# A six-layer decoder on one Trainium2 core: reordered turns in two 16-head attentions, whole projections, and stage ends run beside the next stage

## The chip, the cores and the metric

The kernel is one program on one core of a Trainium2 chip. Its metric is the device time of one execution in microseconds (us), as the median of three runs; lower is better.

A core has five engines with queues of their own: TensorE (PE, with weight loads shown as PEld), VectorE (DVE), ScalarE (ACT), GpSimd (POOL) and SyncE (SP, which here only issues DMAs). Each works through its own list of instructions in a fixed order; they meet through semaphores. PE's results go to PSUM, which the kernel divides into eight banks of 128 x 512 fp32.

## The reference

All is fp32, with eight sequences of 256 tokens and 256 features. Six sublayers follow each other, each as `x = layernorm(x + f(x))`:

1. a gated convolution and state layer; 2. a cross attention, 16 heads of 64, over 77 context rows; 3. a mixture of eight experts (two per token) with a shared one; 4. a self-attention, 16 heads of 16, with rotary position; 5. a cross attention as 2; 6. a self-attention, 16 heads of 16, with two key sets:

```python
sim = (qg_n[None, None] * q_n).sum(-1).mean(-1)
sim = (sim - sim.min()) / (sim.max() - sim.min())
pos = sim > 0.9
...
x_pos = masked_attn(pos)
x_neg = masked_attn(~pos)
reg_out = (x_pos[:, :REG] + x_neg[:, :REG]) * 0.5
tok_out = jnp.where(pos[:, :, None, None], x_pos[:, REG:], x_neg[:, REG:])
```

The first five tokens (`REG`) are registers. The minimum and the maximum of `sim` are over tokens, so the last attention's masks need every token of sublayer 5.

## The kernel before

The change touches sublayers 4 to 6. Tensors stay in SBUF, batch by batch (b = 0 to 7, 256 tokens), as rows (`x_s`) and turned (`xT_s`).

**A scheduler and hand-written order.** The program is written as a trace of instructions; a scheduler fixes each engine's list beforehand from its own estimates. `tc.issue_after(ins)` keeps what is written inside behind `ins` on the same engine. In the two 16-head attentions PE's order is so bound by hand (`bound`); in the cross attention and between stages the scheduler chooses.

**Heads16** is shared by sublayers 4 (`Rotary`) and 6 (`split`). One turn i handles one of four groups of four heads of a batch, 32 turns in all. Its four heads' matmuls have 32 rows each and lie on four strips of the array (`tile_position`). In turn i:

- `scores(i)` (L1032): queries times keys into two bank pairs; DVE takes the row maxima (L1038).
- `products(i-2)` (L1080): exponentials times values, with sums of them in a spare column, into the bank `op`; ACT copies it out (L1087).
- place 0: the first half of a projection, of values or of an output block, in the bank `mm`.
- `exponentials(i-1)` (L1061): scores again, turned, with the maximum subtracted through a spare row; ACT's exp (L1069).
- place 1: the second half of that block; place 2: a side block in `op`, which DVE empties (turning a finished batch, L89 and L94, or the register tokens' steps, L1496, L1520, L1530).
- `turn_maxima(i)` (L1048): the maxima turned into `op`; DVE adds them to the queries (`shifted`, L1188 or L1403).
- place 3: copies out of `mm`, and DVE's and POOL's work on older turns.

PSUM holds one `op`, one `mm` and three bank pairs `sc`, taken in turn by scores and exponentials. For the division, `products` sends the sums by DMA into a compact 128 x 16 tile (`comp`, L1091), `inverted` takes the reciprocal (L1098) and sends it back (L1100), and `normed` spreads and multiplies it (L1108 to L1112). The output block of batch b stands at turn 4b+10 (4b+8 for the last).

**Rotary** projects batch b+1 while batch b is attended (turns 4b, 4b+1, 4b+3) and turns a finished batch two turns after its output. When all turns are through, its pools close.

**cross** begins with keys (L375, L384, L446), values, weighted keys (L457) and weighted values (L411), and then goes through 16 units of scores (L476), turning (L505) and outputs (L521). What a stage leaves over is handed to the next one as a list `tail` of pieces.

**Signs** gathers, after each batch of the second cross attention, `sim` from a projection (L1343) and a power on POOL (L1357). `positive` takes the extremes over the tokens: DVE reduces along the rows, POOL across the partitions:

```python
nc.vector.tensor_reduce(e2, ext, AX.X, ALU.max)
e3 = s1.tile([P, 2], F32, name="e3")
nc.gpsimd.partition_all_reduce(e3, e2, P, bass_isa.ReduceOp.max)
```

**split** (sublayer 6) starts with 15 "early" blocks (queries, keys, values of five batches) in `sc` banks, ACT copying half of the queries (L1435) and DVE the other half (L1438); the signs are turned (L1645), stored to DRAM and spread from there by small DMAs (`marked`, L1454) into spare rows of queries and keys. The other three batches are projected in turns 8 to 19.

Of the kernel before, what the change touches and what calls it, by code (L numbers as in the profile page):

```python
# [18 lines left out]
P = 128  # L19
# [31 lines left out]
def decoder_kernel(ctx: ExitStack, tc: tile.TileContext, a: dict, out: bass.AP):  # L51
# [281 lines left out]
    def cross(xs, W, bias, ctxT, at_unit, after, tail):  # L333
# [10 lines left out]
        with ExitStack() as st:  # L344
            c1 = st.enter_context(pool_of(tc, name="c1", bufs=1))
# [208 lines left out]
            places = (1, 1, 4, 5, 5, 6, 6)  # L554
# [397 lines left out]
    class Heads16:  # L952
# [12 lines left out]
        def __init__(self, st, queries, keys, shifted):  # L965
# [19 lines left out]
            nc.gpsimd.tensor_scalar(self.second, self.second, cs["slot"][:, 1:2], None, ALU.add)  # L985
            self.qs, self.pT, self.o, self.comp, self.oT = ({} for _ in range(5))
# [14 lines left out]
        def project(self, w, col, xT_b, ps, halves=(0, 1)):  # L1001

            for c in halves:
                for kc in range(2):
                    nc.tensor.matmul(  # L1005
                        ps[:, c * SEQ : (c + 1) * SEQ],
                        w[:, kc, col + c * P : col + (c + 1) * P], xT_b[:, kc, :],
                        start=kc == 0, stop=kc == 1,
                    )

        def values(self, xT_b, wv, ps, halves=(0, 1)):
            for kb in halves:
                for kc in range(2):
                    nc.tensor.matmul(
                        ps[:, kb * D : (kb + 1) * D], xT_b[:, kc, kb * P : (kb + 1) * P],
                        wv[:, kc, :], start=kc == 0, stop=kc == 1,
                    )
# [56 lines left out]
        def products(self, i):  # L1074
# [9 lines left out]
            if m == 0:  # L1084
                self.o[b, c] = self.c2.tile([P, 2, SEQ], F32, tag="o", name="o")
            o = self.o[b, c]
            nc.scalar.copy(o[:, m], ps[:, :SEQ])  # L1087

# [16 lines left out]
        def normed(self, b, c):  # L1105
            o = self.o.pop((b, c))
            wide = self.c2.tile([P, SEQ], F32, tag="wide", name="wide", bufs=1)
            nc.vector.stream_shuffle(wide, self.rows[c], [i // 16 * 16 for i in range(32)])  # L1108
            nc.vector.copy_predicated(o[:, 0], self.second.bitcast(U32), o[:, 1])
            if c == 0:  # L1110
                self.oT[b] = self.c2.tile([P, 2, SEQ], F32, tag="oT", name="oT")
            nc.vector.tensor_tensor(self.oT[b][:, c], o[:, 0], wide, ALU.mult)  # L1112

        def out(self, oT, w, ps, halves=(0, 1)):
            for j in halves:
# [11 lines left out]
        def run(self, events):  # L1127
# [12 lines left out]
            for i in range(max(max(e[0] for e in events) + 1, n + 2)):  # L1140
                if i < n:
                    bound(self.scores, i)
                with tc.issue_after(self.last.ins):
                    if 0 <= i - 2 < n:
                        bound(self.products, i - 2)
                    for f in events.get((i, 0), ()):
                        bound(f)
                    with ExitStack() as st:
                        if 0 <= i - 1 < n:
                            st.enter_context(  # L1150
                                tc.issue_after(bound(self.exponentials, i - 1).ins)
                            )
                        for f in [*events.get((i, 1), ()), *events.get((i, 2), ())]:
                            bound(f)
                        if i < n:
                            bound(self.turn_maxima, i)
                        for f in events.get((i, 3), ()):
                            f()


    class Rotary:
# [34 lines left out]
        def project(self, b, i, ps, halves=(0, 1)):  # L1196
            self.at.project(self.W[0], i * 256, self.xT_of(b), ps, halves)
# [25 lines left out]
        def values(self, b, ps, halves=(0, 1)):  # L1223
            self.at.values(self.xT_of(b), self.W[1], ps, halves)
# [18 lines left out]
        def run(self, st, bias, tail):  # L1243
            at, xs, done, sums, banks = self.at, self.xs, [], {}, {}
            at.open(st)
            events = {}

            def put(i, place, f, *args):
                events.setdefault((i, place), []).append(lambda: f(*args))

            def halves(i, f, *args):

                def half(h):
                    if h == 0:
                        banks[i] = at.mm()
                    f(*args, banks[i], (h,))

                for h in range(2):
                    put(i, h, half, h)

            def emptied(i, f, *args):
                put(i, 3, lambda: f(*args, banks.pop(i)))

            def turn_out(b, ps, copy=None):
                s, half = divmod(b, 2)
                transposed(
                    ps, done[s][0][:, half * 2 : half * 2 + 2, :], done[s][1], half, copy
                )
# [11 lines left out]
            def finish(b):  # L1280
# [3 lines left out]
                normed(sums.pop(b), done[s][0][:, half * 2 : half * 2 + 2, :], nc.gpsimd)  # L1284

            for b in range(NB):
                t = 4 * b
                for c in range(2):
                    put(t + 4 + 2 * c, 3, at.inverted, b, c)
                    put(t + 5 + 2 * c, 3, at.normed, b, c)  # L1290
                put(t + 7, 3, biased, b)
                o = t + (10 if b < NB - 1 else 8)
                halves(o, lambda b, ps, h: at.out(at.oT[b], self.W[2], ps, h), b)
                emptied(o, added, b)
                put(o + 1, 3, finish, b)
                if b < NB - 1:
                    put(o + 2, 2, lambda b: turn_out(b, at.side(), nc.vector.tensor_copy), b)
                n = b + 1
                if n < NB:
                    for k, i in ((0, 1), (1, 0)):  # L1300
                        halves(t + k, self.project, n, i)
                        emptied(t + k, self.projected, n, i)
                        put(t + k + 1, 3, self.rotate, n, i)
                    halves(t + 3, self.values, n)
                    emptied(t + 3, self.valued, n)
            for k, piece in enumerate(tail):
                put(k, 2, lambda piece: piece(at.side(), nc.vector.tensor_copy), piece)
            at.run(events)
            return done, [lambda ps: turn_out(NB - 1, ps)]


    class Signs:
# [49 lines left out]
        def positive(self):  # L1362
# [11 lines left out]
            nc.vector.tensor_reduce(e2, ext, AX.X, ALU.max)  # L1374
            e3 = s1.tile([P, 2], F32, name="e3")
            nc.gpsimd.partition_all_reduce(e3, e2, P, bass_isa.ReduceOp.max)
# [10 lines left out]
    def split(xs, W, bias, signs, cs, tail):  # L1387
        wqkv, wo = W
        wv = wqkv[:, :, 512:768]
        with ExitStack() as st:  # L1390
# [33 lines left out]
            def project(b, i, ps, halves=(0, 1)):  # L1424
                at.project(wqkv, i * 256, xT_of(b), ps, halves)

            def projected(b, i, ps):
                v = ps.rearrange("p (c t) -> p c t", c=2)
                if i == 1:
# [8 lines left out]
                nc.vector.tensor_scalar(  # L1438
                    qms[b][:, 1], v, cs["scaled"][:, 1:2], None, ALU.mult
                )  # L1440

            def values(b, ps, halves=(0, 1)):
                at.values(xT_of(b), wv, ps, halves)
# [5 lines left out]
            def marked(tile, b, k0):  # L1449


                for m in range(2):
                    for k in range(2):
                        nc.sync.dma_start(  # L1454
                            out=tile[at.free[m] + 1 + k :: 32, m],
                            in_=sgr[k0 + k : k0 + k + 1, b].partition_broadcast(4)
                            .to_broadcast([4, 2, SEQ]),
                        )
# [11 lines left out]
            def mark_queries(b):  # L1470
                marked(qms[b], b, 0)

            def mask(b):

                marked(kps[b % 2], b, 2)
# [17 lines left out]
            def registers_scores(b):  # L1493
                qd, sc = rg[b], at.side()
# [22 lines left out]
            def registers_turn(b):  # L1517
                sl, tr = rg[b][0], at.side()
# [7 lines left out]
            def registers_products(b):  # L1526
                pn, vn, on = rg.pop(b), vns.pop(b), at.side()
# [36 lines left out]
            events = {}  # L1564

            def put(i, place, f, *args):
                events.setdefault((i, place), []).append(lambda: f(*args))

            def halves(i, f, *args):

                def half(h):
                    if h == 0:
                        banks[i] = at.mm()
                    f(*args, banks[i], (h,))

                for h in range(2):
                    put(i, h, half, h)

            def emptied(i, f, *args):
                put(i, 3, lambda: f(*args, banks.pop(i)))  # L1580

            for b in range(NB):
                t = 4 * b
                put(t, 2, registers_scores, b)
                put(t, 3, registers_exponentials, b)
                put(t + 1, 3, registers_normed, b)
                put(t + 2, 2, registers_turn, b)
# [290 lines left out]
```

## Time and profile before

| | us |
|---|---|
| median of three runs (1419.97 to 1421.14) | 1420.35 |
| the profiled execution | 1418.84 |
| its span | 1417.1 |
| PE busy | 1337.2 (94%) |
| DVE busy | 784.0 (55%) |
| ACT busy | 490.9 (35%) |
| POOL busy | 423.7 (30%) |

The span runs from the first to the last instruction of the profiled execution. In lines of the timeline the columns are start and length in us, engine, line of the kernel, operation, what is written from what with partitions x elements, the number of instructions put together, and in brackets the idle time before them with what ended it. PE's ends are modelled, so distances between starts are the safer reading.

### The profile page before, as it was taken

To read this page: it belongs to the slowest core of one execution; us is meant where nothing else is said; L and a number is where in the kernel's file an instruction comes from. 1 tells how busy PE (TensorE), PEld (TensorE's weight loads), DVE (VectorE), ACT (ScalarE), POOL (GpSimd) and SP (SyncE) were. 2 spreads that over 40 slices of the span, in tenths; PEclk is the share of its full clock that TensorE was granted. 3 is DMA by queue.
4 is the path that set the end of the run, shared out by engine and by line. 5 is a ranking of instruction groups with operands and counts; after the bars stand their busy time and mean duration, and the time that the engine had idled before them with its cause. 6 is when DMAs were issued, how large, how long until landed. Compare 5 with 4: busy or idle time off the path is not lost.

```text
span 1417.1 us, 21778 instructions
## 1 busy us (share of the span) xinstructions
PE 1337.2 (94%) x8518; PEld 916.2 (65%) x8518; DVE 784.0 (55%) x1505; ACT 490.9 (35%) x734; POOL 423.7 (30%) x470
## 2 busy tenths in 40 slices
PE   8999999999999999999989999799999987999884
PEld 3555578888866666656556665578887875555552
DVE  3776465555643223324657777455655653766773
ACT  3455633243331022221134444343233312444441
POOL 0100012131200133246335575412453452122422
PEclk9999999999999999999999999999999998999996
DMA  8000053335240022242120000043222200000000
GB/s 277 6 1 0 1 165 91 107 91 159 96 193 0 24 74 89 79 138 67 38 83 3 3 3 3 2 156 109 88 74 78 71 0 12 15 21 16 23 11 23
DMA packets 80201, 88.22 MB, mean 62 GB/s; under 512 B 14564, under 2 KB 74884, under 8 KB 79588
## 3 DMA queue, kind: packets, MB, share of 16 engines
q1 hardware_dynamic: 76692, 77.53, 17.4%
q0 software_dynamic: 3408, 9.31, 2.3%
q8 instruction: 68, 1.11, 0.3%
q14 instruction: 33, 0.27, 0.1%
HBM read 56.77 MB, written 29.52 MB: 61 GB/s over the span
## 4 chain that ended last, share of the span: by engine, by line
PE 71%; DVE 6%; POOL 3%; issue 2%; DMA 2%; ACT 1%; SPq 0%; another core or an unknown queue 0%; POOLq 0%; DVEq 0%; ACTq 0%
PE mm L521 9%; PE sc L476 8%; PE mm L779 7%; PE ps_sc L1032 5%; PE mm L842 5%; PE ps_sc L1061 5%; PE op L1080 4%; PE tr L796 3%; PE ps_mm L1117 3%; PE ps_mm L1005 3%; PE tr L856 2%; PE sc L505 2%; PE sc L375 2%; PE sc L457 2%; PE sc L411 2%
## 5 line engine op out<-in xcount | busy, mean ns | idle before, releaser
L1038 DVE TENSOR_REDUCE mx<-ps_sc 128x4 f32<-128x1024 f32 x128 | 150.8, 1221 | 39.2 <-PE ps_sc L1032 39.1
L1069 ACT ACTIVATE pT<-ps_sc 128x1024 f32<-128x1024 f32 x128 | 124.1, 1021 | 97.0 <-PE ps_sc L1061 97.0
L496 POOL TENSOR_TENSOR p<-p,sm 128x616 f32<-128x616 f32 x60 | 72.7, 1217 | 242.9 <-DVE sm L493 216.3
L521 PE MATMUL mm<-Ub,pT 128*128 128x256 f32 (+1 forms) x640 | 144.6, 379 | 0.5 <-ACT pT L75 0.4
L476 PE MATMUL sc<-M,xT_s 128*128 128x308 f32 x512 | 138.9, 423 | 1.1 <-ACT pT L75 1.1
L521 PEld LDWEIGHTS mm<-Ub,pT 128*128 128x128 f32 (+1 forms) x640 | 120.8, 190 | 20.0 <-ACT pT L75 0.9
L779 PE MATMUL mm<-xT_s,w 128*128 128x512 f32 x256 | 115.1, 602 | 3.3 <-DVE h L785 3.3
L476 PEld LDWEIGHTS sc<-M,xT_s 128*128 128x128 f32 x512 | 94.4, 188 | 35.3 <-ACT pT L75 2.1
L489 ACT ACTIVATE p<-p 128x616 f32<-128x616 f32 x64 | 45.9, 717 | 154.4 <-DVE p L485 132.7
L779 PEld LDWEIGHTS mm<-xT_s,w 128*128 128x128 f32 x256 | 48.4, 192 | 58.2 <-issue 54.2
L1061 PE MATMUL ps_sc<-qs,kp 32*128 32x256 f32 x1024 | 82.9, 411 | 0.6 <-DVE mx L1038 0.6
L816 POOL DMA_INDIRECT xb<-xd,token x39 | 37.3, 956 | 146.2 <-PE tr L823 81.0
L1080 PE MATMUL op<-pT,va 128*32 128x256 f32 x1024 | 74.4, 405 | 5.0 <-DVE qs L1188 2.2
L483 DVE TENSOR_REDUCE nmx<-sc 128x8 f32<-128x616 f32 x64 | 51.1, 799 | 46.2 <-PE sc L476 46.2
L842 PE MATMUL mm<-wE,xbT 128*128 x156 | 73.5, 593 | 0.3 <-ACT xbT L828 0.3
L1061 PEld LDWEIGHTS ps_sc<-qs,kp 32*128 32x128 f32 x1024 | 52.9, 189 | 28.4 <-issue 23.9
L114 POOL TENSOR_SCALAR rstd<-mv 128x2 f32<-128x2 f32 x48 | 11.8, 245 | 175.2 <-DVE mv L112 175.2
L492 DVE TENSOR_REDUCE sm<-p 128x8 f32<-128x616 f32 x64 | 50.6, 790 | 22.2 <-ACT p L489 21.9
L1087 ACT COPY o<-op 128x256 f32<-128x256 f32 x64 | 23.8, 372 | 111.7 <-PE op L1080 111.7
L181 PE MATMUL pair<-xT_s,w 128*128 128x512 f32 x128 | 57.9, 612 | 0.9 <-DMA w<-in_W_inT 0.9
L254 PE MATMUL pair<-xc,w 128*128 128x512 f32 x128 | 58.6, 600 | 0.0
L828 DVE COPY hT<-tr 128x256 f32<-128x256 f32 x39 | 16.6, 425 | 75.7 <-PE tr L823 75.7
(293 smaller groups left out, 2459.3 us busy)
## 6 DMA issues: line engine op xcount, KB each, us to landing
Ub<-ud SPq DMA_DIRECT2D x32, 512.0 KB
ud<-U SPq DMA_DIRECT2D x16, 616.0 KB
wE<-in_wE SPq DMA_DIRECT2D x4, 1536.0 KB
yd<-y SPq DMA_DIRECT2D x39, 128.0 KB
Ub<-ud SPq DMA_DIRECT2D x32, 104.0 KB
ud<-U SPq DMA_DIRECT2D x4, 608.0 KB
x_s<-in_x SPq DMA_DIRECT2D x8, 256.0 KB
w<-in_Wo SPq DMA_DIRECT2D x2, 1024.0 KB
```

The source lines that it names most:

```text
L181: last = nc.tensor.matmul(ps[:, i, :], w_in[:, kc, c * P : (c + 1) * P], xT_s[:, kc, :], start=kc == 0, stop=kc == 1,)
L254: last = nc.tensor.matmul(ps[:, i, :], w_dt[:, kc, c * P : (c + 1) * P], xc[s][kc // 2][:, kc % 2, :], start=kc == 0, stop=kc == 3,)
L476: nc.tensor.matmul(sc[:, a, : 4 * NCTX], xT_b[:, kc, j * P : (j + 1) * P], M[:, a * 4 : a * 4 + 4, kc, at : at + NCTX], start=kc == 0, sto ...
L496: engine.tensor_tensor(pv, pv, bcast(sm, 2, [P, 8, NCTX]), ALU.mult)
L521: nc.tensor.matmul(o[:, j * D : (j + 1) * D], pT[:n, c, j * P : (j + 1) * P],  Us[b][:n, g, c], start=g == 0 and j == 0 and c == 0, stop=g ...
L779: nc.tensor.matmul(ps, w[:, kc, cols], xT_s[:, kc, :], start=kc == 0, stop=kc == 1)
L842: nc.tensor.matmul(ps, xT[:, kc, :], column(j, kc * 512, 512), start=kc == 0, stop=kc == 1)
L1032: nc.tensor.matmul(scs[s // 2][:, s % 2, qb * SEQ : (qb + 1) * SEQ], self.queries(b, c, s, m)[:, qb * P : (qb + 1) * P], self.keys(b, c, s ...
L1038: self.last = nc.vector.tensor_reduce(self.mx[m][:, :, 2 * j : 2 * j + 2, self.free[m]].rearrange("p q s -> p s q"), scs[j].rearrange("p s ...
L1061: nc.tensor.matmul(scs[s // 2][:, s % 2, kb * SEQ : (kb + 1) * SEQ], self.keys(b, c, s, m)[:, kb * P : (kb + 1) * P], qs[s * 32 : (s + 1) ...
L1069: last = nc.scalar.activation(pT[:, 2 * j : 2 * j + 2].rearrange("p s k t -> p s (k t)"), scs[j], AF.Exp)
L1080: nc.tensor.matmul(ps[s * 32 : (s + 1) * 32, :SEQ], va[:, kb, 8 * c + 2 * s + m, :], pT[:, s, kb, :], start=kb == 0, stop=kb == 1, tile_po ...
```

## The change

It does these things:

- **Order within a turn**: scores, products, exponentials, the side block (now place 0), a whole block in `mm` (place 1), maxima, then copies and the rest (place 2). The halves go.
- **What falls after the last turn** is not run in further turns but returned, with the step that closes the rotary pools, as pieces for the cross attention to run: three after its first keys, three after its first values, the last after the first weighted values. The cross attention's first pool lies at the other end of SBUF (`side="right"`), and `o`, `oT`, `wide` in a pool that stays open.
- **The last batch's division** in both attentions goes without DMA: the sums are copied where they lie, a reciprocal is taken of 128 x 256, and the shuffle fetches them from the other half of each 32 rows.
- The output of batch 6 stands at turn 32, not 34; the rotary's last batch is scaled by DVE, not POOL; its turned copies are DVE's.
- **Signs**: the extremes across partitions come from a PE transpose, a DVE maximum, and a matmul with ones that spreads them.
- **split**: another order of the early blocks, with the tail's two pieces and the signs' two steps between them; early queries copied by ACT alone; the marking DMAs of one batch and half for queries and keys together, first half first; projections of the last three batches at turns 5, 9, 13; 11, 15, 17; 19, 21, 23.

The core of the diff:

```diff
@@ Heads16.products / normed
+            if b == NB - 1:
+                return
...
+                rows = self.rows[c]
+                nc.vector.tensor_copy(rows, o[:, 1])
+                nc.vector.copy_predicated(rows, second, o[:, 0])
+                nc.vector.reciprocal(rows, rows)
+                nc.vector.stream_shuffle(wide, rows, [(i + 16) % 32 for i in range(32)])
@@ Heads16.run
-            for i in range(max(max(e[0] for e in events) + 1, n + 2)):
+            for i in range(n + 2):
                 if i < n:
                     bound(self.scores, i)
-                with tc.issue_after(self.last.ins):
+                with tc.issue_after(self.last.ins), ExitStack() as st:
                     if 0 <= i - 2 < n:
                         bound(self.products, i - 2)
-                    for f in events.get((i, 0), ()):
-                        bound(f)
...
+                    if 0 <= i - 1 < n:
+                        st.enter_context(tc.issue_after(bound(self.exponentials, i - 1).ins))
+                    for f in work.pop((i, 0), ()):
+                        bound(f, self.side())
+                    ends = []
+                    for f, end in work.pop((i, 1), ()):
+                        ps = self.mm()
+                        bound(f, ps)
+                        ends.append(lambda end=end, ps=ps: end(ps))
+                    if i < n:
+                        bound(self.turn_maxima, i)
+                    for f in ends + work.pop((i, 2), []):
+                        f()
+            rest = []
...
+            return rest
@@ Rotary.run, and split likewise
-                o = t + (10 if b < NB - 1 else 8)
+                o = t + (10 if b < NB - 2 else 8)
...
+            return done, rest[:-1] + [lambda ps: close(), rest[-1]]
@@ Signs.extremes, positive
+            nc.tensor.transpose(ps[:2, :P], e2, ident)
+            most = s1.tile([P, 1], F32, name="most")
+            nc.vector.tensor_reduce(most[:2], ps[:2, :P], AX.X, ALU.max)
...
+            nc.tensor.matmul(ps[:, :2], ones[:2], self.both[:2], start=True, stop=True)
             e3 = s1.tile([P, 2], F32, name="e3")
-            nc.gpsimd.partition_all_reduce(e3, e2, P, bass_isa.ReduceOp.max)
+            nc.vector.tensor_copy(e3, ps[:, :2])
@@ split
+            at_turn = ((5, 9, 13), (11, 15, 17), (19, 21, 23))
...
+            turn_last, add_last = tail
+            for i in range(3):
+                early(0, i)
+            fill(0)
+            turn_last(at.mm())
+            early(1, 0)
+            add_last(at.mm())
+            for i in range(1, 3):
+                early(1, i)
+            fill(1)
+            for i in range(3):
+                early(2, i)
+            early(3, 0)
+            signs.extremes(at.side())
+            early(3, 1)
+            pos = signs.positive(at.side())
...
+            early(3, 2)
...
+            for b in range(2):
+                mask(b, True)
@@ the second cross attention
-            lambda b, n_s, nT_s, ps: signs.add(b, nT_s, ps), tail,
+            lambda b, n_s, nT_s, ps: signs.add(b, nT_s, ps), tail, (0, 0, 0, 1, 1, 1, 4), "right",
```

## The prediction

> **What bounds the kernel now.** I read the page first (PE is busy for 94% of the span and has 71% of the chain that ended last), then the busy times by stretch, then the list of PE's waits, then the timeline of single turns and of the three places where one stage hands over to the next. The stretches are: rotary turns, start of the second cross attention, its end with the start of the last attention, the last attention's turns, the end.
>
> ```profile
> 712.00:912.00 200.00, 183.85 (x1874) 116.95 (x1875) 139.43 (x257) 85.39 (x118) 103.60 (x111) 0.98 0.06 17
> 912.00:950.00 38.00, 36.88 (x311) 31.22 (x310) 19.22 (x31) 16.76 (x25) 12.43 (x10) 1.00 0.33 105
> ...
> 1148.00:1210.00 62.00, 50.00 (x256) 38.61 (x258) 21.70 (x46) 14.81 (x26) 18.82 (x18) 0.86 0.03 9
> 1210.00:1390.00 180.00, 161.63 (x1716) 99.16 (x1720) 125.65 (x246) 77.92 (x114) 51.17 (x73) 0.97 0.07 16
> 1390.00:1417.00 27.00, 10.91 (x48) 6.14 (x48) 6.84 (x21) 2.59 (x4) 4.52 (x6) 0.63 0.09 29
> ```
>
> The columns are stretch, length, busy time of PE, PE's loads, DVE, ACT, POOL, then PE's granted clock, DMA share and GB/s. PE idles 16 us in the rotary turns, 12 and 18 us in the last attention, 16 us at the end, and where it idles its clock falls (0.86, 0.63), so idle time is paid twice.
>
> A turn on PE, from start to start, is scores S (L1032), products P (L1080), exponentials E (L1061), maxima turned T (L1048), and in some turns a matmul block M (projection, values or output) and a side block X. I number turns by the starts of L1032 and take lengths from one start to the next. In the rotary turn that begins at 780.27 (turn 12, 6.93 long):
>
> ```profile
> 783.41 1.15 PE L1061 MATMUL ps_sc<-qs,kp 32*128 32x256 f32 x16
> ...
> 785.45 0.60 PE L89 MATMUL op<-ident,x_s 128*128 128x128 f32 x4
> 786.09 0.69 DVE L94 COPY xT_s<-op 128x512 f32<-128x512 f32 x1 [2.12 <-PE op L89]
> ...
> 786.84 0.44 PE L1048 MATMUL op<-ident,mx 128*128 128x128 f32 x2 [0.79 <-DVE xT_s L94]
> ```
>
> T needs the one `op` bank, which DVE must first empty, so 1.38 us pass from X to T (PE's waits name this xT_s nine times, 8.6 us). And turn 28, without M:
>
> ```profile
> 876.15 1.51 PE L1061 MATMUL ps_sc<-qs,kp 32*128 32x256 f32 x16
> 877.60 0.66 PE L89 MATMUL op<-ident,x_s 128*128 128x128 f32 x4
> ```
>
> Here E takes 1.45 from start to start, not 1.08: its second bank pair is the first one of S, and DVE's first maximum (1.22 us, begun 0.03 after S ends) is not done when only P (1.00) lies between. A half M (1.06) before E covers that today. Behind a waiting E stand X, M and T on PE, and ACT's exponentials.
>
> **Order within a turn and whole projections.** Before: S 1.08, P 1.00, half M 1.06, E 1.08, half M 0.97, X, T 0.31. After: S, P, E, X, whole M, T. A whole M is 1.83 (713.79 to 715.62, eight matmuls together), 0.20 less than two halves. E loses its cover and takes 1.45.
> Turn with M alone: before 5.49; after 1.08+1.00+1.45+1.83+0.31 = 5.67, so +0.18. Turn with X and M: before 6.93; after X lasts 0.50 and DVE empties it under M: 5.67+0.50 = 6.17, so -0.76. X alone or neither: unchanged (5.33, 4.02).
> Rotary: 20 turns of the first kind, +3.6; five with both (3, 12, 16, 20, 24), -3.8; turn 1, -0.2; turn 0 waits for DVE either way. Sum -0.4. Bounds: +4 if M covers nothing more, -2 if E hardly waits.
>
> **Last attention's turns.** Its projections also move, from turns 8 to 19 (three of each four) to 5, 9, 11, 13, 15, 17, 19, 21, 23; nine before and after. By turn, before to after: 5 and 21, 4.02 to 5.67 (+3.3 together); 8, 12, 16 keep only X, 6.88 to 5.13 (-5.3); 9, 13, 17, 5.60 to 5.67 (+0.2); 10, 14, 18, X with output, 6.85 to 6.17 (-2.0); 11, 15, 19, X with M, where DVE finishes the normalisation only 6.2 into the turn, as now (-0.2); 22, 26, 30, 7.25 to 6.17 (-3.2); 23 gets M, 6.33 to 6.62 (+0.3); 24 ran at half clock after the idle turn 23 (6.40 against 5.13), which M now fills (-1.3); 6, +0.2. Sum -8.0. Bounds: -4 if half of the `op` waits come back (PE's waits for nsl, pn and od total 19.5 there), -10 if turn 28's half clock (6.37) goes too.
>
> **Rotary end.**
>
> ```profile
> 902.36 0.37 ACT L1087 COPY o<-op 128x256 f32<-128x256 f32 x1 [1.16 <-PE op L1080]
> ...
> 908.96 2.93 PE L1117 MATMUL ps_mm<-w,oT 128*128 128x256 f32 x6 [3.17 <-DVE oT L1112]
> ```
>
> The last batch's sums go by two DMA trips to be inverted; PE waits and then runs at half clock. From the last P's end (902.3) to the first cross scores (927.7) pass 25.4 us. After: output 6 lies in turn 32, before the last P (901.6: 895.57 + P 1.0 + E 1.65 + X 0.5 + output 1.9 + P 1.0, as the clock is low until 898.7). Then follow on PE, by their lengths from 912.4 on, keys 3.35, turning 6 0.6, values 3.1, output 7 1.83, weighted keys 4.6, weighted values 3.5, turning 7 0.6: 17.6, to 919.2. That is -8.5. I take -7, since turning 6 needs x of batch 6 (bn, rstd on POOL, two scales of 1.23 there: about 906), 1 us after the keys end. Bounds: -3 (values stay behind that wait, so nothing overlaps, and the shorter chain below leaves 2.5 and a little clock) and -9 (no stall, no half clock).
> The last batch's new chain on DVE: copy, two predicated copies, shuffle, product at 0.43 each, and a reciprocal of 128x256. The rows have 0.198 at 8 columns and 0.242 at 16, 5.5 ns a column, so an estimate of 1.6: 3.7 in all against 6.2 now (902.73 to 908.90), below the 6.5 of keys and values that hide it. [...] Eight small DMAs leave SP's queue. The final scale of batch 7 moves from POOL (2.44) to DVE (0.75).
>
> **Start of the last attention.**
>
> ```profile
> 1174.41 0.42 DVE L1365 TENSOR_TENSOR dot<-dot,ssq 128x256 f32<-128x256 f32 x1 [6.00 <-POOL ssq L1357]
> ...
> 1176.24 6.53 PE L1005 MATMUL ps_sc<-xT_s,w 128*128 128x256 f32 x16 [3.93 <-DVE qm L1438]
> ...
> 1181.45 0.15 DVE L1378 TENSOR_TENSOR rng<-e 128x1 f32<-128x1 f32 x1
> ...
> 1197.06 1.15 PE L1032 MATMUL ps_sc<-kp,qm 32*128 32x256 f32 x16 [1.97 <-DMA kp<-sgd]
> ```
>
> DVE stands in the signs' chain behind POOL's power (5.4), the early queries' second half stands behind it on DVE, and PE waits 3.93 and then runs 16 matmuls in 6.53 instead of 3.45. After: those halves are on ACT (0.69 each; ACT has 2.6 us a batch, PE 5.2, so it is hidden), and PE goes on. Early blocks are 1.73. Three end near 1159.5; x of batch 7 comes at 1160.9 as now; turning, one block and the sign matmuls end at 1165.6; POOL's power ends about 1173.4, the pair of extremes about 1176. Six blocks end at 1176 too. Two transposes' worth (0.3), two small DVE steps (0.4), a block (1.73), a matmul and a copy give the maximum at 1178.8, against 1181.45: 2.8 where the POOL reduction takes 4.5 (1176.93 to 1181.45). The extremes' transposes wait for DVE, and behind them on PE stand the last five early blocks. [...] Then come the signs, 1.85 (1181.45 to 1183.30); now their two transposes wait in PE's queue until 1189.5, afterwards only one block (1.73) is ahead. The store goes at 1182 and is readable 1.5 later, as now (1190.59 to 1192.10); only four marking DMAs of 0.57, not six, stand before the first scores' last one; with 1.4 to land, S starts at 1187.2. PE's own work ends there as well. Gain 9.9; I take -10. Bounds -5 (the extremes' transposes hold PE up while POOL works, 5 us, as DVE does now) and -11.
>
> **End.** The output of batch 6 moves two turns up, under the last exponentials; the final chain after 1396.29 takes 3.7 + 0.4 instead of 7.3. That is -3.2; up to half may be lost, as output 6 now stands before the last P, at a half clock that stretches its eight matmuls from 1.9 to 3.7: -2, bounds 0 and -4.
>
> Sum: -0.4 -8 -7 -10 -2 = -27.4. The profiled execution took 1418.84 (span 1417.1 and 1.7 around it): 1391.4. The median of the three runs lies 1.5 above it, so I say 1393.
>
> **Rivals.** (a) The turns gain, the hand-overs hardly: a list of instructions fixed beforehand puts a waiting one (turning 6, extremes) ahead of ready ones, as it did at 1174.41. Turns -8.4, hand-overs -3 and -4, end 0: 1418.8 - 15.4 + 1.5 = 1405. For it: the 6.00 wait is just that. Against: in 912 to 928 PE was never idle.
> (b) Slower: E, now only 1.00 behind S, waits for DVE whenever a maximum starts late. If DVE finishes one 0.69 step first in each of 62 turns, that costs 43 us: 1393 + 43 = 1436. It decides from 27.4/62 = 0.44 us a turn. Against: maxima begin 0.02 to 0.04 after S in nearly every turn, the worst 0.23, after the queries' half on DVE, which stays in three turns.
> (c) The change doesn't do what it says: the keys' tiles wait until the rotary ones are free (0), POOL's power still sets the first scores (0), and the turns stand at their worse bounds (+4 and -4); only the end's -2 is left, 1418.3. A difference under 0.2% (2.8 us) is about what a measurement of this kernel can't tell from none. Against: the waits that leave PE idle in 1148 to 1210 are named (x_s 3.3, qm 3.9, kp 2.0 of 12), and the diff touches what stands behind two of them.
>
> **How the numbers follow.** Forecast 0.70; (a) 0.19; (b) 0.06; (c) 0.05, of which 0.03 within 0.2% and 0.01 to each side. So faster is 0.70+0.19+0.01 = 0.90, same 0.03, slower 0.06+0.01 = 0.07. All good bounds together (-2 -10 -9 -11 -4 = -36) give 1384, all bad ones (+4 -4 -3 -5 = -8) 1412; they seldom come together, so the range is 1384 to 1406, which takes in (a) and leaves out (b), (c) and the worst of the forecast.
>
> **What would show it.** Right: rotary turns with a projection 5.65 to 5.7 long, E 1.45 in all; no wait of T for xT_s where a projection follows; the last attention's first scores at 1197 - 7.4 - 10, near 1180; reciprocal of 128x256 near 1.6. Wrong: E above 1.6, a gap on PE over 2 us around keys or extremes, or first scores of the cross attention later than 922.

## The result and the profile after

The kernel after took 1398.9 us (median of four runs, 1394.38 to 1399.27), the kernel before 1420.16 beside it: ratio 0.9847, 95% interval 0.9821 to 0.9874. The forecast was 1393, its range 1384 to 1406. The profiled execution took 1399.1 (span 1397.3) where the sum had said 1391.4.

The five stretches of before, in the busy times by stretch of the kernel after, cut at the starts of scores: rotary turns, rotary end, start of the last attention, its turns, the end. Columns as before: stretch, length, PE, PE's loads, DVE, ACT, POOL, granted clock, DMA share, GB/s.

```profile
710.40:888.30 177.90, 173.15 (x1755) 118.01 (x1754) 128.72 (x228) 82.31 (x111) 93.70 (x97) 0.98 0.07 19
888.30:924.90 36.60, 30.73 (x288) 23.18 (x287) 21.66 (x47) 13.30 (x21) 15.27 (x18) 0.91 0.01 4
1151.60:1188.30 36.70, 31.43 (x139) 25.81 (x137) 11.30 (x30) 13.63 (x23) 19.43 (x20) 0.95 0.01 2
1188.30:1363.00 174.70, 164.03 (x1730) 105.85 (x1730) 127.56 (x239) 79.12 (x114) 47.69 (x73) 0.96 0.07 19
1363.00:1397.30 34.30, 16.13 (x123) 9.97 (x122) 17.12 (x43) 5.00 (x7) 9.43 (x11) 0.75 0.07 23
```

Idle time and a low clock are now at the two handovers and at the end. In the rotary turns PE is idle for 5 us of 178. Below, "half clock" means a stretch in which the granted clock is 0.5.

The next table has the same cuts in every profile, worked out from the timelines' starts of L1032 (scores), L476 (first cross scores) and L1005 (first early block): from the first scores of turn 0 to those of turn 31, on to the first cross scores, from the first early block to the last attention's first scores, on to its turn 31, and on to the end. The last column is the median of the runs, the others are one execution. The kernel before, measured again on each of the four occasions, had medians of 1419.15 to 1421.12, so medians of two occasions that differ by 2 us say nothing.

| kernel | rotary turns | rotary end | start of last | last's turns | end | median |
|---|---|---|---|---|---|---|
| before | 177.40 | 38.36 | 42.85 | 183.47 | 36.53 | 1420.16 |
| after | 177.97 | 36.55 | 36.74 | 174.66 | 34.37 | 1398.90 |
| e1 order only | 175.41 | 42.14 | 41.30 | 172.43 | 34.59 | 1410.01 |
| e2 close first | 175.42 | 43.10 | 36.11 | 174.61 | 34.52 | 1405.24 |
| e3 DMA division | 175.44 | 33.44 | 36.53 | 173.80 | 36.02 | 1396.36 |
| e4 POOL maximum | 175.41 | 35.29 | 39.64 | 169.83 | 34.76 | 1401.17 |
| e5 half on DVE | 175.40 | 35.05 | 39.81 | 169.79 | 34.41 | 1397.86 |
| e6 divide behind | 178.06 | 32.23 | 36.97 | 174.66 | 31.66 | 1392.47 |
| e7 memsets on DVE | 177.98 | 36.35 | 32.42 | 174.78 | 34.78 | 1395.34 |
| e8 halves round E | 173.20 | 35.57 | 35.91 | 174.55 | 35.71 | 1394.13 |
| e10 = e6 + e7 | 177.98 | 33.17 | 33.16 | 170.84 | 31.38 | 1387.49 |
| e9 = e6 + e7 + e8 | 173.20 | 31.88 | 34.05 | 174.36 | 31.32 | 1383.89 |
| e11 filled start | 178.14 | 35.03 | 36.87 | 172.85 | 34.37 | 1396.11 |
| e12 = e9 + e11 | 173.21 | 31.88 | 33.38 | 169.68 | 32.91 | 1382.14 |

The turn that was shown of before, in the timeline of after (start, length, engine, line, and in brackets the idle time before it and what ended it):

```profile
781.07 1.15 PE L1032 MATMUL ps_sc<-kp,qr 32*128 32x256 f32 x16
...
782.14 1.07 PE L1080 MATMUL op<-pT,va 128*32 128x256 f32 x16
...
783.14 1.52 PE L1061 MATMUL ps_sc<-qs,kp 32*128 32x256 f32 x16
...
784.59 0.66 PE L89 MATMUL op<-ident,x_s 128*128 128x128 f32 x4
785.09 1.89 PE L1005 MATMUL ps_mm<-xT_s,w 128*128 128x256 f32 x8
785.29 0.69 DVE L94 COPY xT_s<-op 128x512 f32<-128x512 f32 x1 [0.52 <-PE op L89]
786.82 0.38 PE L1048 MATMUL op<-ident,mx 128*128 128x128 f32 x2
```

From 781.07 to the next scores at 787.13 are 6.06 us, before 6.93. DVE empties `op` at 785.98, under the projection, and T waits for nothing. E takes 1.45 from start to start (783.14 to 784.59). (X is the side block, M the whole projection, T the maxima, as in the prediction.)

The rotary end, timeline of after:

```profile
893.79 0.43 DVE L1116 COPY_PREDICATED rows<-second,o 128x256 f32<-128x256 uint32 x1
894.26 1.75 DVE L1117 RECIPROCAL rows<-rows 128x256 f32<-128x256 f32 x1
...
895.92 0.38 DVE L1207 SCALAR_TENSOR_TENSOR qs<-qr,cst,op 128x256 f32<-128x256 f32 x1
...
896.45 1.93 PE L1080 MATMUL op<-pT,va 128*32 128x256 f32 x16 [4.04 <-DVE qs L1207]
...
898.32 2.09 PE L1061 MATMUL ps_sc<-qs,kp 32*128 32x256 f32 x16
```

The new division of the last batch's first half stands on DVE ahead of turn 31's shift (`qs`, L1207). PE waits 4.04 for the shift, then products take 1.93 and E 2.09 instead of 1.07 and 1.15: the granted clock is at half from 895.8 to 902.6.

The start of the last attention, timeline of after:

```profile
1155.42 1.84 POOL L970 MEMSET va<- 128x1024 f32 x2
...
1157.23 0.22 POOL L114 TENSOR_SCALAR rstd<-mv 128x2 f32<-128x2 f32 x1
...
1158.41 2.40 DVE L117 TENSOR_SCALAR x_s<-r,mv,rstd 128x256 f32<-128x256 f32 x2 [4.96 <-POOL rstd L115]
...
1161.25 2.87 PE L1005 MATMUL ps_sc<-xT_s,w 128*128 128x256 f32 x8
...
1163.91 2.65 PE L1360 MATMUL ps_mm<-w,xT_s 128*128 128x256 f32 x8
...
1176.76 0.19 DVE L1392 TENSOR_REDUCE e<-ext 128x2 f32<-128x32 f32 x1
...
1179.54 0.16 DVE L1409 TENSOR_TENSOR rng<-e 128x1 f32<-128x1 f32 x1
...
1188.30 1.15 PE L1032 MATMUL ps_sc<-kp,qm 32*128 32x256 f32 x16 [1.51 <-DMA kp<-sgd]
```

Between POOL's power (till 1155.48) and the last batch's rstd lie two memsets that in before ran at 1139.8, and the two scales on DVE take 2.40 where before took 1.04. PE waits for x (2.79 and 0.87), and half clock follows (1162.0 to 1165.4), in which the next two blocks take 2.87 and 2.65 instead of 1.89. The signs' maximum takes 2.59 from 1176.95 to 1179.54.

The end, timeline of after:

```profile
1368.89 1.75 DVE L1117 RECIPROCAL rows<-rows 128x256 f32<-128x256 f32 x1
1370.56 0.23 DVE L1574 TENSOR_TENSOR od<-op,cst 128x128 f32<-128x128 f32 x1
...
1370.85 0.69 PE L1048 MATMUL op<-ident,mx 128*128 128x128 f32 x2 [3.27 <-DVE od L1574]
...
1384.20 3.49 PE L1127 MATMUL ps_mm<-w,oT 128*128 128x256 f32 x8 [4.69 <-DVE oT L1589]
```

The same division stands ahead of `od` here; T waits 3.27 for it, in before 1.52.

### The profile page after: what moved, and what is told of

Its sections match the earlier page's. It is cut to its first block, busy times and chain, and to the rows that moved or that the text cites. A ratio compares the mean times of both kernels' runs of the same rounds, so it can differ in the third digit from the quotient of the medians.

```text
span 1397.3 us, 21759 instructions
## 1 busy us (share of the span) xinstructions
PE 1335.6 (96%) x8521; PEld 928.5 (66%) x8521; DVE 793.6 (57%) x1514; ACT 496.5 (36%) x738; POOL 420.7 (30%) x467
## 4 chain that ended last, share of the span: by engine, by line
PE 71%; DVE 6%; POOL 3%; issue 2%; DMA 2%; SPq 0%; ACT 0%; POOLq 0%; DVEq 0%; ACTq 0%
PE mm L521 9%; PE sc L476 8%; PE mm L778 7%; PE ps_sc L1061 6%; PE ps_sc L1032 5%; PE mm L841 5%; PE op L1080 4%; PE tr L795 4%; PE ps_mm L1005 2%; PE tr L855 2%; PE ps_mm L1127 2%; PE sc L505 2%; PE sc L375 2%; PE sc L411 2%; PE sc L457 1%
## 5 line engine op out<-in xcount | busy, mean ns | idle before, releaser
L476 PE MATMUL sc<-M,xT_s 128*128 128x308 f32 x512 | 139.0, 423 | 1.1 <-ACT pT L75 1.1
L476 PEld LDWEIGHTS sc<-M,xT_s 128*128 128x128 f32 x512 | 94.4, 188 | 35.3 <-ACT pT L75 2.1
L1061 PE MATMUL ps_sc<-qs,kp 32*128 32x256 f32 x1024 | 99.4, 417 | 0.9 <-DVE mx L1038 0.9
L1061 PEld LDWEIGHTS ps_sc<-qs,kp 32*128 32x128 f32 x1024 | 64.9, 192 | 35.9 <-issue 26.6
L1080 PE MATMUL op<-pT,va 128*32 128x256 f32 x1024 | 71.3, 398 | 4.6 <-DVE qs L1207 4.0
L117 DVE TENSOR_SCALAR x_s<-r,mv,rstd 128x256 f32<-128x256 f32 x66 | 26.0, 436 | 60.9 <-POOL rstd L115 60.9
```

The source lines that it names most:

```text
L476: nc.tensor.matmul(sc[:, a, : 4 * NCTX], xT_b[:, kc, j * P : (j + 1) * P], M[:, a * 4 : a * 4 + 4, kc, at : at + NCTX], start=kc == 0, sto ...
L1061: nc.tensor.matmul(scs[s // 2][:, s % 2, kb * SEQ : (kb + 1) * SEQ], self.keys(b, c, s, m)[:, kb * P : (kb + 1) * P], qs[s * 32 : (s + 1) ...
L1080: nc.tensor.matmul(ps[s * 32 : (s + 1) * 32, :SEQ], va[:, kb, 8 * c + 2 * s + m, :], pT[:, s, kb, :], start=kb == 0, stop=kb == 1, tile_po ...
```

## The experiments

**One part alone, and one part undone.** e1 gives the kernel before the order of after (projections and values stay at their old turns, and divisions, handovers and signs are the old ones):

```diff
-                    for f in events.get((i, 0), ()):
-                        bound(f)
                     with ExitStack() as st:
...
-                        for f in [*events.get((i, 1), ()), *events.get((i, 2), ())]:
-                            bound(f)
+                        for place in (2, 0, 1):
+                            for f in events.get((i, place), ()):
+                                bound(f)
```

> The kernel before with the new order within a turn alone (exponentials right behind products, side block, then both halves together); projections stay at turns 8 to 19, and stage ends, division and signs are untouched. Theory (the order makes nearly all of the turns' gain, the new turns of the projections none): last attention from first scores to turn 31 falls from 183.5 to about 174 (turns 8, 12, 16 to 6.3, 10, 14, 18 and 22, 26, 30 to 5.84, 11, 15, 19 to 6.56), rotary 177.1 to about 177.5, the rest unchanged: some 1411. Rival (the projections' new turns made it): the last attention gains 2 at most and the time is 1418.

1410.01 us (ratio 0.9926, 0.9904 to 0.9949): 10 of the 21 us. The last attention's turns gain 11.0, in after 8.8; after's profile has 3.4 us more of half clock there. So the order gives that gain. Where the projections stand gives at most the 1.3 of turn 24, which still runs at half clock in e1 (6.41, in after 5.13). The theory had the rest unchanged, but the rotary end becomes 3.8 longer: the turning of batch 6 now stands on PE ahead of output 7, and waits for POOL in the row

```profile
905.21 0.33 PE L89 MATMUL op<-ident,x_s 128*128 128x128 f32 x1 [4.54 <-POOL x_s L117]
```

of e1's timeline. Output 7 ends 24.7 us into the stretch, in before 22.6, and the last turning waits behind it. Order and handover belong together here: the order alone loses at the handover.

e2 takes the overlap out of after: what is left of the rotary attention is finished before cross attention's first keys, which keep their place on the right.

```diff
                 rest = at.run(work)
-            return done, rest[:-1] + [lambda ps: close(), rest[-1]]
+                for f in rest[:-1]:
+                    f(at.mm())
+            close()
+            return done, rest[-1:]
...
```

> The changed kernel, but all that is left of the rotary stage is run and its pools are closed before the cross attention's first keys. Theory (the overlap works, and its gain was eaten by a longer wait before it): from turn 31 to the first cross scores 36.5 becomes 39 to 40, time about 1402. Rival (the overlap itself gives nothing, keys and values wait for the rotary tiles): under 1 us, 1399.

1405.24 (0.9897, 0.9872 to 0.9922), and the rotary end 43.10 against 36.55, more than the theory's 39 to 40. The overlap is worth 6.55 (in e2 PE waits 4.03 for x of batch 6, and the stretch has 6.8 us more of half clock). So a gain of the forecast's size was there, and something beside it took 5.

e3 divides the last batch through the two DMA trips again:

```diff
-            if b == NB - 1:
-                return
...
-            if b < NB - 1:
-                nc.vector.stream_shuffle(wide, self.rows[c], [i // 16 * 16 for i in range(32)])
-            else:
...
+            nc.vector.stream_shuffle(wide, self.rows[c], [i // 16 * 16 for i in range(32)])
...
```

> The changed kernel with the last batch's division in both attentions by DMA and a 128x16 reciprocal again. Theory (the 1.75 us reciprocal of the first half stands on DVE ahead of the last queries' shift, so half of the gain is lost there): at the rotary end PE's wait for qs falls from 4.0 to 2.2 and keys hide the DMAs, 1.5 less; at the kernel's end the chain is 2.5 longer, but the wait for od falls from 3.3 to 1.5: in all -1 to +1, 1398 to 1400. Rival (the division without DMA is what shortened both ends): 2 or more at each, 1403.

1396.36 (0.983, 0.9801 to 0.986). The rotary end falls by 3.1, to 33.44, twice what the theory had: PE's wait for the shift is 2.21 again, and half clock lasts 3.4 us there, not 6.8. The DVE division is what that stage lost. The kernel's end grows by 1.65, since the trips have no cover there; its timeline:

```profile
1379.77 3.75 PE L1117 MATMUL ps_mm<-w,oT 128*128 128x256 f32 x8 [8.79 <-DVE oT L1578]
```

After waits 4.69 at that place. The median alone, 2.5 below after's, decides nothing.

**The signs.** e4 gives POOL the maximum over partitions again:

```diff
-            nc.tensor.transpose(ps[:2, :P], e2, ident)
...
+            nc.gpsimd.partition_all_reduce(self.e3, e2, P, bass_isa.ReduceOp.max)
```

> The changed kernel with the signs' extremes taken across partitions by POOL again, at the same place. Theory (TensorE's path is 2.6 from e to the range, POOL's was 4.5, and the first scores wait for the signs): first scores about 1.9 later, time 1401. Rival (PE's early blocks set the first scores anyway): under 0.5, 1399.

```profile
1179.26 0.33 DVE L1401 TENSOR_TENSOR rng<-e 128x1 f32<-128x1 f32 x1 [5.44 <-POOL e L1394]
...
1181.09 0.40 PE L1682 MATMUL ps_mm<-ident,sg 128*32 128x128 f32 x2 [3.59 <-DVE sg L1676]
```

In its timeline DVE waits 5.44 for POOL's result and PE 3.59 behind it; the stage is 2.9 longer, with 3.4 us more of half clock behind PE's wait. e5 puts the second half of the early queries back on DVE (`projected(b, i, ps)` without `False`):

> The changed kernel with the second half of the early queries on DVE again instead of ACT. Theory (that half stood behind POOL's power on DVE and held PE up, 3.9 us and then half clock, and this is most of the gain at the start of the last attention): PE waits 2 to 4 us for qm again, time 1402 to 1405. Rival (the new order of the blocks alone avoids it): under 1, 1399.

```profile
1172.63 0.42 DVE L1383 TENSOR_TENSOR dot<-dot,ssq 128x256 f32<-128x256 f32 x1 [5.58 <-POOL ssq L1374]
...
1176.03 1.99 PE L1005 MATMUL ps_sc<-xT_s,w 128*128 128x256 f32 x8 [2.47 <-DVE qm L1470]
```

The old picture is back in e5's timeline: DVE waits for POOL's power, the queries stand behind it, PE waits 2.47; the stage is 3.07 longer. Yet both medians (1401.17, 1397.86) can't be told from after's, and e5's theory of 1402 to 1405 isn't met. The last attention's turns are 4.8 shorter in both profiles: behind the first scores they have no half clock, after has 10.2 us of it. By the phase of the clock I mean where such stretches of half clock fall in an execution (two expectations further on call the stretches the clock's windows). How much of it there is differs between executions of one kernel: two of e5's four runs took 1394.2 and 1394.3 at a mean clock of 0.989, two 1401.4 and 1402.2 at 0.983. What the start loses, the phase gave back in the profiled ones.

**The two places that the forecast missed.** e6 issues the last batch's first division behind turn 31's shift:

```diff
             self.shifted(b, c, m, qs, ps[:, :SEQ])
+            self.shift = self.newest(mybir.EngineType.DVE)
...
+            late = b == NB - 1 and c == 0
+            with tc.issue_after(self.shift) if late else nullcontext():
+                self.divided(b, c)
```

> The changed kernel with the first half of the last batch's division kept behind the shift of turn 31 on DVE, in both attentions. Theory (that division in front of the shift is what ate the gain at the rotary end): PE's wait for qs falls from 4.0 to 2.2 at the rotary end and the one for od from 3.3 to 1.5 at the kernel's end, 1.8 each and a little clock: 1395. Rival (what follows waits for ACT or for x of batch 6 anyway): under 1, 1398.5.

```profile
893.94 0.47 DVE L1213 SCALAR_TENSOR_TENSOR qs<-qr,cst,op 128x256 f32<-128x256 f32 x1
...
894.56 1.07 PE L1081 MATMUL op<-pT,va 128*32 128x256 f32 x16 [1.94 <-DVE qs L1213]
...
895.14 1.75 DVE L1123 RECIPROCAL rows<-rows 128x256 f32<-128x256 f32 x1
```

1392.47 (0.9807, 0.9791 to 0.9823). In its timeline PE waits 1.94, not 4.04, and what follows runs at full clock; the rotary end falls by 4.3, the kernel's end by 2.7. By the medians one reordered group of instructions on DVE gives 6.4 us. Part of the 4.3 is the half clock that e6 escapes at the rotary end; in e10 below, which has 3.4 us of it there, the rotary end is still 3.4 shorter.

e7 lets DVE write the constants that `Heads16.__init__` writes (seven memsets of va, mx, rows and second, and a sum into second) for the last attention:

```diff
-                nc.gpsimd.memset(va, 1.0)
+                engine.memset(va, 1.0)
...
-            at = Heads16(st, queries, keys, shifted)
+            at = Heads16(st, queries, keys, shifted, nc.vector)
```

> The changed kernel with the memsets that open the last attention's heads on DVE instead of POOL. Theory (with the cross attention's pool at the other end of SBUF they wait for its second pool, fall between POOL's power and rstd of batch 7, and slow DVE's scales beside them): rstd 1.8 earlier, scales 0.4 each instead of 1.1 and 1.3, x of batch 7 about 3 earlier, first scores 2 to 3 earlier: 1396. Rival (POOL's power sets it all): under 0.5, 1399.

```profile
1153.99 0.91 DVE L970 MEMSET va<- 128x1024 f32 x1 [0.16 <-DVE mv L112]
...
1156.29 0.23 POOL L114 TENSOR_SCALAR rstd<-mv 128x2 f32<-128x2 f32 x1
...
1157.35 1.28 DVE L117 TENSOR_SCALAR x_s<-r,mv,rstd 128x256 f32<-128x256 f32 x2 [2.13 <-POOL rstd L115]
...
1159.07 1.89 PE L1005 MATMUL ps_sc<-xT_s,w 128*128 128x256 f32 x8
```

1395.34 (0.9817, 0.979 to 0.9844). The scales take 1.28 for 2.40, the block behind them 1.89 for 2.87, and the stage is 4.3 shorter: 32.42, within 0.5 of the forecast (42.85 less 10).

Not all of the 4.3 belongs to the edit. The block behind x starts 1.80 earlier, counted from the stage's first block. The half clock that after has there costs 1.7, and e7 has none. And the first marking DMA follows the store by 2.37 us in after (1182.14 to 1184.51) but by 1.52 in e7 and before; with the same code this gap was 1.52 to 2.71 in other executions. At equal half clock (3.4 us) and an equal gap (1.52), e9 below, with the edit, has a start of 34.05, e2 and e8, without it, 36.11 and 35.91: 2.0 are sure.

e8 gives M back its two halves, one on each side of E, with X still directly behind E:

```diff
+                    for f, end in work.pop((i, 1), ()):
+                        ps = self.mm()
+                        bound(f, ps, (0,))
...  (exponentials, then the side block)
+                    for f, ps in blocks:
+                        bound(f, ps, (1,))
```

> The changed kernel with the matmul block in halves round the exponentials again, the side block staying ahead of the second half. Theory (E's uncovered wait costs 0.37 and the whole block saves 0.20, so a turn with a block is 0.18 too long): turns with a block alone 5.67 to 5.49, about 27 of them, turns with both 6.06 to about 6.0 and 5.84 to about 5.8: -5, time 1394. Rival (half a block no longer covers DVE's emptying of the side bank, and T waits again): the turns with both grow by 0.3 each, in all -1, 1398.

```profile
774.79 1.13 PE L1014 MATMUL ps_mm<-w,xT_s 128*128 128x256 f32 x4
775.85 1.15 PE L1061 MATMUL ps_sc<-qs,kp 32*128 32x256 f32 x16
776.93 1.13 PE L1014 MATMUL ps_mm<-w,xT_s 128*128 128x256 f32 x4
777.89 0.38 PE L1048 MATMUL op<-ident,mx 128*128 128x128 f32 x2
```

E takes 1.08 again (775.85 to 776.93), a turn with M alone 5.54 (772.67 to 778.21) for 5.67, and from turn 4 to the start of turn 31 it is 148.22 for 150.93. So the whole projections cost 2.7 us there; the other 2.0 that its rotary turns gain are half clock in turn 1. 1394.13 (0.9821, 0.9802 to 0.9839); its last attention has the same length as in after, with one more stretch of half clock in it.

**Do the repairs add?** e10 is e6 and e7 together, e9 those and e8.

> The kernel after with two edits that were measured alone: the last batch's first division is issued behind turn 31's shift, and the last attention's constants are written by DVE instead of POOL. My theory, that these two places are where the forecast's missing 9 us stood (rotary end -1.8 for -7, start of the last attention -6.1 for -10): the two gains are in different stages and add, -4.3 at the rotary end, -2.7 at the end, -4.3 at the start of the last attention, so 1399 - 11 = 1388 (1386 to 1390), with the rotary end at 32.2 and the start of the last attention at 32.4. The rival, that what those runs gained was the phase of the clock's windows: the gains don't add, one of the two stages falls back to its length after (36.6 or 36.7), and the time is 1392 to 1395.

> The same two edits, and the matmul block again in two halves around the exponentials, as before, with the side block still between them. My theory, that E's wait of 0.4 in turns without a side block costs 20 times some 0.13 in the rotary turns: turns 4 to 31 at 148.2 instead of 150.9, everything else as without it, so 1388 - 2.7 = 1385 (1383 to 1387.5). The rival, that whole projections are right and the halves only shift the clock's windows: turns 4 to 31 at 150.9 and 1388 or above.

They add: e10 1387.49 (0.9786, 0.977 to 0.9801) for 1388, e9 1383.89 (0.9751, 0.973 to 0.9772) for 1385. In both, rotary end, start and end hold their gains within 1.7 us; from turn 4 to turn 31 e9 takes 148.22 again. The part of e7's gain that may be half clock and store stays in this sum: e9's start is 1.6 longer than e7's.

**The half clock at the last attention's start.** e11 puts a block of eight unread matmuls ahead of its first scores, and another in turn 0:

```diff
+            put(0, 1, (lambda ps, *h: values(EARLY - 1, ps, *h), lambda ps: None))
...
             registers_queries(0)
+            values(EARLY - 1, at.mm())
```

> The kernel after with 16 matmuls of work that nobody reads: a block like the early values one (8 matmuls, 1.83 us) ahead of the last attention's first scores, where PE idles 1.51, and another in turn 0 ahead of T, where it idles 2.00. My theory, that turns 0 to 2 (5.04, 6.03, 6.18 us) are long because PE idles 3.9 us and then runs 10.2 us at half clock: the first scores come 0.3 later, turn 0 stays near 5, turns 1 and 2 fall to 4.4 to 5.2, the last attention's turns from 174.7 to 171 or 172.5, and the time is 1395.5 to 1397.5. The rival, that those turns wait for DVE and the store and not for the clock: the granted clock rises and the turns stay as they are, 1399 to 1401, as the added blocks come on top.

Busy times in three stretches there, of after and then of e11:

```profile
1190.00:1195.00 5.00, 3.00 (x22) 1.93 (x23) 3.09 (x5) 0.60 (x2) 0.57 (x3) 0.77 0.13 39
1195.00:1200.00 5.00, 4.53 (x30) 2.50 (x30) 2.85 (x4) 1.94 (x2) 0.48 (x1) 0.50 0.13 40
1200.00:1205.00 5.00, 4.66 (x50) 2.19 (x42) 2.66 (x3) 1.05 (x2) 0.00 (x0) 0.70 0.04 11
```

```profile
1190.00:1195.00 5.00, 4.24 (x33) 2.74 (x30) 3.60 (x6) 0.60 (x2) 0.55 (x2) 1.00 0.14 38
1195.00:1200.00 5.00, 4.46 (x38) 2.78 (x42) 3.38 (x6) 1.94 (x2) 0.48 (x1) 0.75 0.14 43
1200.00:1205.00 5.00, 4.48 (x56) 2.33 (x52) 2.25 (x4) 2.31 (x3) 0.00 (x0) 0.91 0.13 34
```

With the idle time filled, the half clock lasts 3.4 us instead of 10.2, and turns 0 to 2 take 15.4 (1188.07 to 1203.50) instead of 17.25, though work was added. Turn 0 stays at 5.01, turn 1 falls to 3.96, turn 2 takes 6.46, as the half clock now lies in it. The median, 1396.11 (0.9828, 0.9814 to 0.9843), is 2.8 below after's, about as much as such medians differ anyway. That the filling did it isn't shown: e4 and e5 have no half clock in these turns without any filling, so a lucky phase is a rival. What speaks for the filling is the mean clock of all five runs of e11, 0.987 or 0.988, where after's four had 0.980 to 0.987.

> The two edits at the handovers, the halves around the exponentials, and the filled start. My theory: what each gave alone adds, 1385 - 2.5 = 1382.5 (1380 to 1386). The rival: with the constants on DVE the early blocks end sooner against the store, PE's idle time ahead of the first scores is other than in the kernel after, and the added blocks only take 1 to 2 us: 1386 to 1388.

e12, all four, takes 1382.14 (0.975, 0.9733 to 0.9766), the fastest here, and not to be told from e9. By the medians it beats the kernel after by 16.8.

## Why the prediction was right or wrong

Against the profiled execution the sum missed by 7.7 us (1391.4 for 1399.1). Term by term, predicted and measured: rotary turns -0.4 and +0.6; rotary end -7 and -1.8; start of the last attention -10 and -6.1; its turns -8.0 and -8.8; end -2 and -2.2; stretches that the change doesn't touch 0 and -1.4. Both handovers gave less than forecast, the rest came out within 1.4. The median, 5.9 above the forecast, lies about half-way to rival (a)'s 1405; that it fell into the range owes something to a range that takes (a) in. Of the signs named beforehand, E and the turns came as the right ones; the first cross scores at 924.86, later than 922, and the last attention's at 1188.30 instead of near 1180, were signs against it.

**Turns: right.** M alone 5.67 predicted, 5.66 to 5.67 measured; X and M 6.17 and 6.06; E 1.45. The +0.6 holds 2.6 us of half clock in turn 1 (8.63, in e1 to e5 6.06), and that is phase: e6, e7, e10 and e11 have it too, e1 to e5 don't, and there the rotary turns are 2.0 shorter than before. That is more than the -0.4 of the sum, since X with M took less than costed, and two of the twenty turns with M alone (7 and 30) were 5.85 before and fell to 5.67. In the last attention X with output took 5.84, predicted 6.17. Its -8.8 compares like with like: the granted clock of these turns is 0.96 in before and in after. Moving the projections was hardly needed for it, as e1 shows.

**Rotary end: the step that failed** is "3.7 in all ..., below the 6.5 of keys and values that hide it". It holds for the second half of the heads, whose product is done at 909.61, under the values. The first half's chain has no keys beside it: it stands in turn 31 between DVE's normalisation and the shift, and PE waits for that shift. I looked for what hides the chain and not for what is queued behind it. PE's wait grew from 2.21 to 4.04, and in the 6.8 us of half clock that follow the five blocks up to the keys (products, E, X, output 6, the last products) took 8.29, where the sum had 6.05 with a little half clock in it. So the keys begin 4.1 later than forecast; about 1 more was lost between them and the scores. e6 brings 4.3 of the 5.2 back.

**Reciprocal.** My estimate from small ones was 1.6, the measured duration 1.75.

**End: right in part by luck.** I had put the loss there down to output 6 at half clock. It took 2.42 from start to start instead of 1.83, but e6 gives 2.7 back by moving the division: the failed step stands here too, ahead of `od`.

**Start: the terms that were mis-sized** are "x of batch 7 comes at 1160.9 as now" and, by less, the store that is "readable 1.5 later, as now". Counted from the stage's first block (1154.2 before, 1151.56 after) the scales of x end 2.0 later than in before, and half clock behind them, which the sum had at nothing, costs 1.7. The store was readable after 2.37, which is 0.85 more and differs between executions. The late x comes from the seven memsets: on POOL they now fall between power and rstd, and into DVE's scales, 16 us later than in before; e7, which takes them off POOL, shows that. Why they moved is read from the diff and not shown, as no run moves the pool alone: it puts the cross attention's pool at the other end of the memory, and the constants seem to wait until that attention's second pool is closed. What a `side` argument does to memsets stood in no line that I costed. e7's start is 4.3 shorter, 2.0 of it surely by the edit. The other steps held: 2.8 for the maximum, 2.59 measured against e4's 5.44, and no queries behind the power. So a transpose on TensorE with a maximum on DVE did the reduction across partitions here, and e4's stage, with POOL's, is 2.9 us longer.

**Rivals.** (a) had the mechanism, a fixed list with the wrong instruction ahead; but it was one that was ready and long, not one that waits, and its 1405 is about as far from the 1398.9 as the forecast is. Its handovers of -3 and -4 were measured as -1.8 and -6.1. e6 shows the mechanism for the rotary end. (b) is refuted: at full clock E costs 1.45 in most turns and at most 1.61, only in turn 1 of each attention 2.6 (e4, e5), and the sum has what this costs. (c) is refuted: keys begin at 904.74, beside the last division, and e2, e4 and e5 each lose 2.9 to 6.6 us in their stage when their part is undone.

## What to carry to other kernels

When work is moved onto an engine, ask two questions: what hides it, and what stands behind it in that engine's list; the second cost 5 us here and one reordering brought 6 back. A tile pool's place in memory can be an edge of the schedule too: by all appearance the memsets that write into the freed space moved with it here. And cost the half clock with a stall on TensorE (at the rotary end 6.8 us of it came with after's wait of 4.04, none with e6's of 1.94), but judge a change by its own stage: a difference of 3 us can vanish in the phase of the clock somewhere else (e5's start was 3.07 longer, its last attention's turns 4.8 shorter).

## What the hardware showed

A scale on DVE took up to 1.34 us beside POOL's work, for 0.41 alone. In after, one scale on DVE begins at 1158.41, while POOL runs memsets, and ends at 1159.54, 0.14 after POOL's last memset (1159.40); the next begins at 1159.46 and ends at 1160.81, 0.15 after POOL's sum (1160.66). In e7, where the two take 1.28 together, they end 0.14 and 0.15 after POOL's instructions. It went the other way too: in before a scale begins at 1160.38, 0.04 after POOL's scaling of the keys, and takes its 0.41, while that POOL instruction takes 0.92 instead of the 0.76 it has in after. What held the two scales of after up for 1.13 and 1.34 us, no run here shows.

In the profiles of before and after the granted clock is at half for 3.4, 6.8 or 10.2 us and nothing between in mid-kernel. The profiled executions of after, e6, e7, e10 and e11 had 6.8 us of it from 717.7 to 719.7 on, those of e2 to e5 none there, with nothing changed ahead of it (rotary turns of 177.97 to 178.14 and of 175.40 to 175.44). Runs of one kernel spread by 0.3% (after, 1394.38 to 1399.27) to 0.6% (e4, 1394.87 to 1403.77), so differences of 3 us between medians were read from the stages alone.
